# Router products placed singly between value products, and other orders in the opening and the first expert, of a gated cross-attention and mixture-of-experts layer in f32

## The chip, the cores and the metric

One core of a Trainium2 chip runs the whole layer in one program. The metric is the device time of one execution in microseconds (us); times of the kernel before are given as the median of three runs, and the profile is of one further execution.

## The reference

The layer has 4096 rows x of 512 features and a context of 3202 rows. First the rows are normalised and attend to the context by a trilinear similarity; the attended rows go through W_qv and are added to x by a gate. Then each row is normalised again, a router picks two of eight experts for it, and each expert is a two-layer network over at most 640 rows. All of it is f32.

```python
Sim  = (q @ w1)[:, None] + (ctx @ w2)[None, :] + (q * w3) @ ctx.T + b_sim   # q = layernorm(x)
hat  = softmax(Sim, axis=1) @ ctx
hbar = softmax(Sim.max(axis=1), axis=0) @ q
x    = x + tanh(g_xattn) * (concat([q, hat, q * hat, q * hbar]) @ W_qv + b_qv)
...
n = layernorm(x)
gates = softmax(n @ w_router + b_router);  topv, topi = top_k(gates, 2)
buf[e, pos] = n[token]        # each expert's rows, first come, up to its capacity
out = gelu(buf @ w1[e] + b1[e]) @ w2[e] + b2[e]
y   = weighted mean of the two experts' rows;  x + tanh(g_ffn) * y
```

## The kernel before

Every matrix product of size goes by the seven products of Strassen and Winograd: sums of blocks are formed on VectorE (DVE), seven products are done on TensorE (PE) into PSUM banks, and their results are combined on DVE and ScalarE (ACT). A function that does so has a chain of products named 1, 6, 7, 5, 2, 4, 3 in that order. The engines run in an order that the tile framework's scheduler records for each of them; `tc.issue_after(x)` holds an instruction behind another in that order, and a DMA belongs to the order of the engine that issues it (SyncE, called SP, for most loads; ACT and GpSimd, called POOL, for some).

**Attention.** Eight groups of 512 rows are worked one after the other. For the first group `stage_a_first` (L183 to L205) loads four tiles of 128 rows, normalises each (`layernorm`, L94: statistics on DVE, the reciprocal root `rstd` on POOL, the norm on DVE), transposes them on PE (L111), copies them by ACT (L192), and scales them into Qp on DVE (L197); `right_sums` (L176 to L179) forms the block sums of the right side. At the kernel's start stand also two iotas on POOL with casts on DVE, `tok` and `sno` (L79 to L86), which are used only in routing and by the experts. `tok_i` and `sno_i` share one buffer.

`stage_s` makes the scores of a group: for each of 7 pairs of context blocks (the last is a pair of 65 rows) the chain at L399, with its products at L453. In the first group `build` (L314) loads each block of the context (ktb, 896 KB with its sums), forms its block sums on DVE and stores it (L327, from ACT) for the other groups, which load it from there. `live["norm"]` (L202) and `live[0]["t2"]` are the instructions behind which these sums are held. The end of stage_s finds the greatest score of each row: transposes of M on PE (mps, L477), the reduction mt, a diagonal matrix dgm, a product with ones (mbps, L155), which puts the maxima along the free dimension of all partitions, and the copy mb on ACT (L495). `stage_e` subtracts mb from the scores (L510) and exponentiates them (L511).

`stage_v` makes the value products (L570). In the first group they are not by the seven products: for each half i of the features and each half h of the context there are 26 products of 512 columns. In between, DVE and POOL work on what later groups need: `build_values` (values' block sums, stored to memory) and `build_weights(c)`, which loads W_qv's parts, forms their sums and stores them, one c after each (i, h). Four products with a column of ones follow (rsps, L655), then the second group's scores (`pas`, `p6s` and so on). `xr`, loaded on SP at the end of stage_v's preparations for `stage_d`, holds rows of x.

**Router products.** Before the first group's values the kernel folds the router's weights into W_qv: for each of the four parts k of W_qv, 16 products of 128x128 with 128x8 (`router_weights`, L250), each of which is two records in the trace, since it is in f32. Part 1 stands before mps, part 2 after mbps, and parts 0 and 3 after all value products. The parts of W_qv lie in buffers lent by others: wq1 in hqT's, wq2 in xr's, wq0 in hs2's and hs4's, wq3 in T2's. The products of parts 1 and 2 go to PSUM bank we12 and those of 0 and 3 to we03; DVE copies them to `we` (L580, L600, L601).

**Routing** (L844 to L1094): products (L912), norms, choice of experts, positions by products with a triangular matrix (L1014), and 64 indirect scatters from POOL (L1045) that put each normalised row in its expert's rows of `buf_d`. `out` is stored by ACT (L920) ahead of the statistic Square (L923).

**Experts** (L1102 to L1322): `expert_in(e)` (L1164) loads five tiles xb of 128 rows from buf_d, each as soon as one of three buffers is free, transposes them on PE (bps, L111), copies them on DVE to bT (L1179), takes each row's factor and token number (dc, cf, ti, L1183 to L1186) and forms the block sums x (L1190 to L1193). The first expert's row loads wait for all scatters. `w1_sums` and `w2_sums` form the weights' block sums w1s (L1126 to L1129) and w2t (L1210 to L1213); `seven` (L1131) does the products pah, p6h, p7h and so on (L1135). `expert_in` and `w1_sums` of the next expert stand in the middle of the one before.

## Time and profile before

| what | value |
|---|---|
| time of the kernel before, median of 3 runs | 2696.91 us (2695.22 to 2697.17) |
| profiled execution, its own time | 2696.22 us |
| span of that execution in the profile | 2694.4 us |
| busy share of PE, DVE, ACT, POOL | 98%, 62%, 17%, 9% |
| mean granted clock of PE in the span | 0.987 |
| mean rate of the DMA | 162 GB/s |

The profile gives the engines' busy times, the span in 40 slices of 67.4 us, the groups of instructions by line with the idle time ahead of them, and who ended it. PEclk and "granted clock" are the share of full speed at which PE was allowed to run. A line of the timeline gives the start from the beginning of the span, the length, the engine, the line in the code, the operation, and the names of the tiles that it writes and reads; x32 at its end says that 32 records in a row were put together, and brackets tell the idle time ahead and what ended it. A matmul in f32 is two records, so 32 records are 16 matmuls. PEld is the load of weights into PE, which may run beside the products.

### The profile page before, as it was taken

How to read it: one execution, taken by the hardware profiler on the slowest of the kernel's cores; microseconds unless marked ns; L12 is line 12 of the kernel's file. 1: busy time of each engine (PE TensorE's matmuls, PEld its weight loads, DVE VectorE, ACT ScalarE, POOL GpSimd, SP SyncE). 2: the span in 40 equal slices, each digit the busy share in tenths (PEclk: the TensorE clock that was granted, in tenths of full speed). 3: DMA queues.
4: the chain of work that ended last, by engine and by line, in shares of the span. 5: the costliest groups of instructions: out<-in, count | busy, mean ns of one | idle time of the engine just before them, and what ended most of it. 6: DMA issues, size and time to landing. Idle time of an engine off the chain costs nothing. (4 is left out here: it accounts for less than half of the span.)

```text
span 2694.4 us, 29935 instructions
## 1 busy us (share of the span) xinstructions
PE 2644.3 (98%) x11388; PEld 2130.5 (79%) x11388; DVE 1671.4 (62%) x3283; ACT 449.6 (17%) x768; POOL 241.0 (9%) x292
## 2 busy tenths in 40 slices
PE   8999999999999999999999996999999999999999
PEld 6748888888888888888888875677777777777776
DVE  7765756845937757559357366564747475655654
ACT  1200200201201102002011043111121111111111
POOL 0210000000000000000000056001001010101010
PEclk9898999999999999999999998999999999999999
DMA  6885765656637647556446694323323132323210
GB/s 260 246 305 187 181 219 153 228 171 165 232 142 178 235 164 193 198 165 214 160 147 198 209 366 148 131 90 121 110 82 126 63 127 100 118 83 106 82 59 20
DMA packets 184051, 436.65 MB, mean 162 GB/s; under 512 B 18616, under 2 KB 85165, under 8 KB 181858
## 3 DMA queue, kind: packets, MB, share of 16 engines
q1 hardware_dynamic: 157538, 357.48, 41.3%
q0 software_dynamic: 16624, 47.37, 5.3%
q10 hardware_dynamic: 9744, 29.87, 2.9%
q8 instruction: 90, 1.47, 0.2%
q14 instruction: 55, 0.45, 0.1%
HBM read 356.22 MB, written 85.60 MB: 164 GB/s over the span
## 5 line engine op out<-in xcount | busy, mean ns | idle before, releaser
L453 PE MATMUL pas<-Qp,kt 128*128 128x256 f32 (+1 forms) x728 | 175.5, 383 | 0.0
L1135 PE MATMUL pah<-bT,w 128*128 128x320 f32 x512 | 161.0, 437 | 0.8 <-DVE bT L1179 0.8
L570 PE MATMUL pbv<-E,vt 128*128 128x256 f32 (+1 forms) x728 | 159.5, 379 | 0.0
L570 PEld LDWEIGHTS pbv<-E,vt 128*128 128x128 f32 (+1 forms) x728 | 138.2, 190 | 18.9
L453 PEld LDWEIGHTS pas<-Qp,kt 128*128 128x128 f32 (+1 forms) x728 | 136.0, 188 | 21.4
L511 ACT ACTIVATE E<-E 128x1024 f32<-128x1024 f32 (+1 forms) x112 | 110.7, 995 | 156.2 <-DVE E L510 154.3
L510 DVE TENSOR_TENSOR E<-E,mb 128x1024 f32<-128x1024 f32 (+1 forms) x112 | 124.7, 1138 | 12.4 <-ACT mb L495 12.4
L1135 PEld LDWEIGHTS pah<-bT,w 128*128 128x128 f32 x512 | 98.0, 192 | 39.9 <-DVE bT L1179 1.2
L1135 PE MATMUL pao<-w,h 128*128 128x256 f32 x512 | 121.0, 379 | 0.0
L1315 POOL DMA_INDIRECT out<-acc,ti x40 | 42.9, 1072 | 861.0 <-DVE acc L1314 861.0
L912 PE MATMUL x1p<-W,q2T 128*128 128x264 f32 x512 | 116.1, 387 | 0.0
L410 ACT COPY p1s<-pas 128x512 f32<-128x512 f32 (+1 forms) x56 | 31.1, 555 | 499.2 <-issue 256.5
L1292 PE MATMUL op<-w,h 128*128 128x512 f32 x256 | 113.7, 592 | 0.0
L471 DVE TENSOR_TENSOR M<-M,E 128x1024 f32<-128x1024 f32 (+1 forms) x96 | 109.0, 1135 | 6.7 <-ACT p1s L410 0.5
L1135 PEld LDWEIGHTS pao<-w,h 128*128 128x128 f32 x512 | 96.7, 190 | 16.7 <-issue 4.3
L912 PEld LDWEIGHTS x1p<-W,q2T 128*128 128x128 f32 x512 | 96.7, 190 | 16.1
L426 DVE TENSOR_TENSOR E<-p4s,u3s 128x512 f32<-128x512 f32 (+1 forms) x56 | 36.5, 652 | 109.8 <-PE p4s L453 109.8
L522 DVE TENSOR_TENSOR SM<-SM,E 128x1024 f32<-128x1024 f32 (+1 forms) x80 | 88.5, 1106 | 0.0
L1292 PEld LDWEIGHTS op<-w,h 128*128 128x128 f32 x256 | 47.2, 190 | 52.0 <-issue 46.4
L453 PE MATMUL p6s<-q,kt 128*128 128x256 f32 (+1 forms) x364 | 87.3, 381 | 0.0
L453 PE MATMUL pbs<-Qp,kt 128*128 128x256 f32 (+1 forms) x364 | 86.6, 379 | 0.0
L453 PE MATMUL pbs<-q,kt 128*128 128x256 f32 (+1 forms) x364 | 86.6, 379 | 0.0
(406 smaller groups left out, 5245.7 us busy)
## 6 DMA issues: line engine op xcount, KB each, us to landing
kt<-kt_d SPq DMA_DIRECT2D x84, 896.0 KB
w<-in_w SPq DMA_DIRECT2D x32, 2048.0 KB
wp<-wt_d SPq DMA_DIRECT2D x56, 520.0 KB
vt<-vs_d SPq DMA_DIRECT2D x28, 896.0 KB
vt<-vs_d SPq DMA_DIRECT2D x28, 640.0 KB
kt_d<-ktb ACTq DMA_DIRECT2D x12, 896.0 KB
buf_d<-zero SPq DMA_DIRECT2D x80, 129.0 KB
xb<-buf_d SPq DMA_DIRECT2D x40, 258.0 KB
```

The lines of the kernel that those rows point to most:

```text
L410: nc.scalar.copy(p1, cut(pa))
L426: tt(done(1, 0), cut(p4), u3, ALU.add)
L453: nc.tensor.matmul(ps[:w, jl, :], kts[j][:, KSLOT[p], k, :], B[p][:, k, :], start=start and jl == 0 and k == 0, stop=stop and k == 1, skip ...
L471: tt(m, m, e[:w, :, h], ALU.max)
L510: live[g]["last"] = tt(e, e, m, ALU.subtract)
L511: live[g]["exp"] = nc.scalar.activation(e, e, AF.Exp)
L522: tt(s, E_t[0][:, lr] if jj == 1 else s, e, ALU.add)
L570: mm = nc.tensor.matmul(ps[b], vt[: WJ[j], j - i * JH, b * P : (b + 1) * P], right(j), start=start and j == 0 and (b == 0 or g == 0), stop ...
L912: mm = nc.tensor.matmul(ps[:, j, :B1], qTs[g][:, c, q * P : (q + 1) * P], W1[:, c, j, :], start=(c == 0), stop=(c == DC - 1))
L1135: nc.tensor.matmul(ps, a, b, start=start and i == 0, stop=stop and i == len(A) - 1, skip_group_check=True)
L1292: nc.tensor.matmul(ps, hT[:, k, 2 * MH :], W2[:, k, :], start=(k == 0), stop=(k == KH - 1))
L1315: sc = nc.gpsimd.indirect_dma_start(out=out[:, :], out_offset=rows_of(ti, s), in_=acc[:, :], in_offset=None, bounds_check=N - 1, oob_is_er ...
```

## The change

The iota and cast of `tok` go to routing, those of `sno` to the beginning of the experts' part. In `layernorm` the statistics are ordered behind the norm of the tile two before, and each tile's root behind that of the one before. Half of the scalings into Qp go to ACT, `live["norm"]` becomes the last scaling of the first two tiles, the first p1 copies are ordered behind the scalings, and the stores of the context blocks stand behind the chain of their pair. The router products become a generator of single products: one is issued after each value product, those of parts 1 and 2 through the first half i and those of parts 0 and 3 through the second, with both banks held from the start of stage_v; `build_weights` is called for no c, 0 and 1, 2, and 3 after the four (i, h). In routing the store of `out` stands behind Square. For the experts the first weight sums come before `expert_in(0)`, whose small operations stand behind them; five row tiles have buffers of their own; and every other copy to bT is done by ACT.

```diff
@@ -76,33 +76,29 @@
-    tok_i = const.tile([P, NT], I32, name="tok_i", tag="tok_i")
-    nc.gpsimd.iota(tok_i, pattern=[[P, NT]], base=0, channel_multiplier=1)
-    tok = const.tile([P, NT], F32, name="tok")
-    nc.vector.tensor_copy(tok, tok_i)
-    sno_i = const.tile([P, E * NST], I32, name="sno_i", tag="tok_i")
-    nc.gpsimd.iota(sno_i, pattern=[[P, E * NST]], base=0, channel_multiplier=1)
-    sno = const.tile([P, E * NST], F32, name="sno")
-    nc.vector.tensor_copy(sno, sno_i)
-
...
+    scales, normed = [], []
+
...
         st = sm.tile([P, 6], F32, name=f"st{t}", tag="st")
-        nc.vector.bn_stats(st, src)
+        with tc.issue_after(normed[-2]) if len(normed) > 1 else ExitStack():
+            nc.vector.bn_stats(st, src)
         mv = sm.tile([P, 2], F32, name=f"mv{t}", tag="mv")
...
         ve = sm.tile([P, 1], F32, name=f"ve{t}", tag="ve")
-        nc.gpsimd.tensor_scalar(ve, mv[:, 1:2], EPS, None, ALU.add)
-        nc.gpsimd.tensor_tensor(rstd, ve, neghalf, ALU.pow)
+        with tc.issue_after(scales[-1]) if scales else ExitStack():
+            nc.gpsimd.tensor_scalar(ve, mv[:, 1:2], EPS, None, ALU.add)
+        scales.append(nc.gpsimd.tensor_tensor(rstd, ve, neghalf, ALU.pow).ins)
         nc.gpsimd.tensor_tensor(sd[:, t : t + 1], ve, rstd, ALU.mult)
-        return nc.vector.tensor_scalar(dst, src, mv[:, 0:1], rstd, ALU.subtract, ALU.mult)
+        nrm = nc.vector.tensor_scalar(dst, src, mv[:, 0:1], rstd, ALU.subtract, ALU.mult)
+        normed.append(nrm.ins)
+        return nrm
@@ -187,19 +183,24 @@
                 nc.sync.dma_start(q, x[t * P : (t + 1) * P, :])
-                nrm = layernorm(sm, q, q, t)
+                layernorm(sm, q, q, t)
                 ps = transposed(ps_tr, q, f"qps{t}")
...
                     for c in range(DC):
-                        ts(Qp[:, c, h], qT[:, c, h], ws[:, 2 * DC + c : 2 * DC + c + 1], ws[:, DC + c : DC + c + 1], ALU.mult, ALU.add)
+                        w3, w2 = ws[:, 2 * DC + c : 2 * DC + c + 1], ws[:, DC + c : DC + c + 1]
+                        if c < DC // 2:
+                            qp = ts(Qp[:, c, h], qT[:, c, h], w3, w2, ALU.mult, ALU.add)
+                        else:
+                            live["qp"] = nc.scalar.activation(Qp[:, c, h], qT[:, c, h], AF.Identity, scale=w3, bias=w2)
+                    if t == 1:
+                        live["norm"] = qp
                 if t == 2:
...
                         nc.scalar.dma_start(bqv, b_qv.partition_broadcast(P))
-            live["norm"] = nrm
             right_sums(0, qT, Qp)
@@ -242,18 +243,20 @@
-            def step(ps, ks, first=True):
+            def products(ps, ks):
+
...
                                     ps[:, k, (f0 // P) + f, :], a[:, d, f * P : (f + 1) * P], wrc[:, d, :],
-                                    start=first and k == ks[0] and f0 == 0 and f == 0 and d == 0, stop=d == DC - 1,
+                                    start=k == ks[0] and f0 == 0 and f == 0 and d == 0, stop=d == DC - 1,
                                     skip_group_check=True,
...
-
-            return step
+                                yield
+
+            return products
@@ -324,7 +327,6 @@
                 tt(A21, A11, A21, ALU.subtract)
-            nc.scalar.dma_start(kt_d[j], kt)
             return kt
@@ -407,7 +409,8 @@
             p1 = tmp("p1")
-            nc.scalar.copy(p1, cut(pa))
+            with tc.issue_after(live["qp"].ins):
+                nc.scalar.copy(p1, cut(pa))
             p6 = bank(f"p6{name}")
@@ -458,6 +461,9 @@
                 e_add = chain(f"s{g}_{jj}", prod, w, nj, lambda i, j: e[:w, j, i, :, :])
+                if g == 0:
+                    for j in js:
+                        nc.scalar.dma_start(kt_d[j], kts[j])
                 m = M[:w, :, :nj, :]
@@ -470,18 +476,14 @@
             if g == 0:
-                rw, rps = router_weights(), we_bank("we12")
-                rw(rps, [1])
+                live[g]["we"] = router_weights()
             ps = ps_tr.tile([P, 4, P], F32, name=f"mps{g}", tag="tr")
...
             ps = ps_tr.tile([P, 4, P], F32, name=f"mbps{g}", tag="tr").rearrange("p a b -> p (a b)")
-            dr = diag_rows(ps, f"m{g}", mt)
-            if g == 0:
-                with tc.issue_after(dr.ins):
-                    rw(rps, [2], False)
+            diag_rows(ps, f"m{g}", mt)
@@ -494,8 +496,6 @@
             live[g]["mt"], live[g]["mb"] = mt, mb
-            if g == 0:
-                live[g]["we"] = rw, rps
@@ -562,7 +562,7 @@
-            def product(ps, what, right, start=True, stop=True):
+            def product(ps, what, right, start=True, stop=True, beside=iter(())):
                 for i in range(2):
@@ -572,33 +572,37 @@
                             )
+                            with tc.issue_after(mm.ins):
+                                next(beside, None)
                 return mm
...
             if g == 0:
-                rw, rps = v["we"]
-                with tc.issue_after(v["last"].ins):
-                    nc.vector.tensor_copy(we[:, 1:3], rps[:, 1:3])
+                ps12, ps03 = we_bank("we12"), we_bank("we03")
+                w12, w03 = v["we"](ps12, [1, 2]), v["we"](ps03, [0, 3])
                 for i in range(2):
...
                     for h in range(2):
-                        vv = product(
-                            ps, (h, i * 256), lambda j: E[j // 2][: WJ[j], :, h, j % 2, :], start=h == 0, stop=h == 1
+                        product(
+                            ps, (h, i * 256), lambda j: E[j // 2][: WJ[j], :, h, j % 2, :], start=h == 0, stop=h == 1,
+                            beside=w03 if i else w12,
                         )
+                        if (i, h) == (0, 1):
+                            assert next(w12, 0) == 0
+                            with tc.issue_after(v["last"].ins):
+                                nc.vector.tensor_copy(we[:, 1:3], ps12[:, 1:3])
                         for j in range(NJ)[(2 * i + h) * 4 : (2 * i + h + 1) * 4]:
...
                         with tc.issue_after(v["last"].ins):
-                            build_weights(2 * i + h)
+                            for c in [[], [0, 1], [2], [3]][2 * i + h]:
+                                build_weights(c)
                         if (i, h) == (0, 1):
...
                         nc.scalar.copy(hqT[:, 2 * i + b, :], ps[b].rearrange("p a b -> p (a b)"))
-                with tc.issue_after(vv.ins):
-                    rps = we_bank("we03")
-                    rw(rps, [0])
-                    rw(rps, [3], False)
-                    nc.vector.tensor_copy(we[:, 0], rps[:, 0])
-                    nc.vector.tensor_copy(we[:, 3], rps[:, 3])
+                assert next(w03, 0) == 0
+                nc.vector.tensor_copy(we[:, 0], ps03[:, 0])
+                nc.vector.tensor_copy(we[:, 3], ps03[:, 3])
                 between()
@@ -869,6 +873,11 @@
+        tok_i = c2.tile([P, NT], I32, name="tok_i")
+        nc.gpsimd.iota(tok_i, pattern=[[P, NT]], base=0, channel_multiplier=1)
+        tok = c2.tile([P, NT], F32, name="tok")
+        nc.vector.tensor_copy(tok, tok_i)
+
@@ -917,12 +926,13 @@
             )
-            nc.scalar.dma_start(out[t * P : (t + 1) * P, :], x1)
             junk = sb.tile([P, D], F32, name=f"jx{t}", tag="jx", bufs=2)
-            nc.scalar.activation(
+            sq = nc.scalar.activation(
                 junk, x1, AF.Square, scale=-float(D), bias=s.sum[:, i : i + 1], accum_out=s.ssd[:, i : i + 1]
             )
+            with tc.issue_after(sq.ins):
+                nc.scalar.dma_start(out[t * P : (t + 1) * P, :], x1)
@@ -1112,6 +1122,11 @@
+        sno_i = cb.tile([P, E * NST], I32, name="sno_i", tag="sno_i")
+        nc.gpsimd.iota(sno_i, pattern=[[P, E * NST]], base=0, channel_multiplier=1)
+        sno = cb.tile([P, E * NST], F32, name="sno", tag="sno")
+        nc.vector.tensor_copy(sno, sno_i)
+
@@ -1126,7 +1141,7 @@
             tt(S4, A12, S2, ALU.subtract)
-            tt(A21, A11, A21, ALU.subtract)
+            return tt(A21, A11, A21, ALU.subtract)
@@ -1161,12 +1176,12 @@
-        def expert_in(e):
+        def expert_in(e, after=None):
             xT = cb.tile([P, DC, CAP], F32, name=f"bT{e}", tag="bT")
...
             for s in range(NST):
-                xb = sb.tile([P, R], F32, name=f"xb{e}_{s}", tag="xb", bufs=3)
+                xb = sb.tile([P, R], F32, name=f"xb{e}_{s}", tag="xb", bufs=NST)
                 ld = nc.sync.dma_start(xb, buf_d[e * CAP + s * P : e * CAP + (s + 1) * P, :])
@@ -1176,14 +1191,16 @@
                 ps = transposed(ps_tr, xb, f"bps{e}_{s}")
-                nc.vector.tensor_copy(xT[:, :, s * P : (s + 1) * P], ps)
+                (nc.scalar.copy if s % 2 else nc.vector.tensor_copy)(xT[:, :, s * P : (s + 1) * P], ps)
...
                 dc = sb.tile([P, 1], F32, name=f"dc{e}_{s}", tag="dc")
-                tt(dc, xb[:, D : D + 1], xb[:, D + 1 : D + 2], ALU.subtract)
-                tt(c, xb[:, D + 3 : D + 4], sno[:, k : k + 1], ALU.is_equal)
+                with tc.issue_after(after.ins) if after else ExitStack():
+                    tt(dc, xb[:, D : D + 1], xb[:, D + 1 : D + 2], ALU.subtract)
+                    tt(c, xb[:, D + 3 : D + 4], sno[:, k : k + 1], ALU.is_equal)
                 nc.vector.scalar_tensor_tensor(c, dc, c, xb[:, D + 1 : D + 2], ALU.mult, ALU.add)
-                nc.vector.tensor_copy(ti[:, s : s + 1], xb[:, D + 2 : D + 3])
+                with tc.issue_after(after.ins) if after else ExitStack():
+                    nc.vector.tensor_copy(ti[:, s : s + 1], xb[:, D + 2 : D + 3])
@@ -1200,7 +1217,7 @@
             S1, S2, S4 = (cb.tile([P, 2, P * KQ], F32, name=f"w1s{k}_{e}_{h}", tag=f"w1s{k}") for k in (1, 2, 4))
-            left_sums(S1, S2, S4, A11, A12, A21, A22)
+            last_sum[0] = left_sums(S1, S2, S4, A11, A12, A21, A22)
             return A11, A12, A22, S1, S2, A21, S4
@@ -1214,10 +1231,11 @@
         stored = []
-        nxt = expert_in(0)
+        last_sum = [None]
+        w1s = w1_sums(0, 0)
+        nxt = expert_in(0, last_sum[0])
         with tc.issue_after(row_loads[-1]):
             load_half(0, 1)
-        w1s = w1_sums(0, 0)
         for e in range(E):
```

## The prediction

> **What bounds it now.** I read the page's busy shares first: TensorE (PE) has 98% of the span, so time can only come out of PE's idle gaps, its slow-clock stretches, or its work. Next the PE rows of the slices.
> ```profile
> span 2694.4 us, 29935 instructions
> PE   8999999999999999999999996999999999999999
> PEclk9898999999999999999999998999999999999999
> ```
> PE dips in slices 1 and 25, the clock in slices 2, 4 and 25: the opening, both ends of the first value products, and routing with the first expert. The view of waits names the gaps (us in total, times, longest):
> ```profile
> PE bps L111 <- DMA xb<-buf_d: 16.2, 1, 16.2
> PE qps L111 <- DVE q L105: 11.2, 2, 10.7
> PE mbps L155 <- DVE dgm L154: 1.5, 1, 1.5
> ```
> The chain of waits follows only the last scatters (12% "issue") and says nothing about these places; PE's own timeline does (start, length, idle before).
> ```profile
> 99.15 3.63 PE L250 MATMUL we<-wrc,wq 128*128 128x8 f32 x32
> 104.78 2.07 PE L155 MATMUL mbps<-dgm,ones 128*128 128x512 f32 x2 [1.51 <-DVE dgm L154]
> 106.65 6.83 PE L250 MATMUL we<-wrc,wq 128*128 128x8 f32 x32
> ...
> 204.90 12.17 PE L250 MATMUL we<-wrc,wq 128*128 128x8 f32 x64
> 216.92 1.84 PE L655 MATMUL rsps<-ones,mb 128*128 128x1 f32 x8
> 218.63 3.76 PE L453 MATMUL pas<-Qp,kt 128*128 128x256 f32 x8
> ```
> The router products are 64 matmuls, each two records: 22.6 us in three runs. In the last, 32 matmuls take 0.38 us each; in the first, 16 take 0.227. The windows say why (stretch, us, busy time of PE, PEld, DVE, ACT, POOL, granted clock, DMA share, GB/s): the clock is halved from 104.1 to 117.8 and from 206.5 to 223.6.
> ```profile
> 104.10:113.30 9.20, 8.52 (x34) 7.49 (x35) 6.71 (x9) 4.81 (x5) 0.38 (x1) 0.50 1.07 350
> 113.30:117.80 4.50, 4.50 (x7) 1.92 (x8) 4.50 (x5) 1.06 (x1) 3.08 (x1) 0.50 1.07 356
> 206.50:216.90 10.40, 10.40 (x51) 10.40 (x51) 3.62 (x10) 0.00 (x0) 1.60 (x3) 0.50 0.79 277
> 216.90:223.60 6.70, 6.70 (x21) 5.71 (x22) 5.80 (x10) 0.59 (x1) 0.66 (x1) 0.50 0.65 242
> 1560.00:1640.00 80.00, 76.03 (x343) 63.29 (x342) 49.24 (x253) 34.51 (x82) 46.69 (x52) 1.00 0.91 337
> ```
> A run of 128x8 products, though PE is "busy" through it, is followed by the half clock.
>
> **The sum** is made against the profiled execution: 2696.22 us, 1.8 outside its span, 0.7 below the median of 2696.91.
>
> **Opening.** Before, the first rstd (POOL, 9.53) stands behind the sno iota, which waits for the tok cast, which DVE does only after the fourth tile's bn_stats (8.52). With the iotas gone the early norms no longer wait for it. The last tile's own chain is bn_stats to 9.21, aggregate 0.18, ve 0.22, rstd 0.56, norm 0.55, with a hand-over of 0.1 to 0.3 between engines; I place its norm at 11.8 instead of 13.62. Then half of the Qp scalings (DVE, 0.33 each, 2.67 us in all) go to ACT, so the first x-sum starts near 15.1 instead of 18.00, and p6, which needs it, at 17.9 instead of 20.1 (its 21.81 less one product of 1.73 that now stands elsewhere in the order): −2.2. From 19.98 to 47.19 PE did 15 products of 1.727, 25.9 us of work in 27.2; the missing 1.3 is one p1 copy that ACT does at 40.80, 18.2 us late, because six kt_d stores of blocks not yet loaded stood before it. In the new order two do, of loaded blocks: −1.3. Together −3.5; between −1.5 (half, if the ktb loads, 896 KB per block, set the pace) and −5.5 (a clock step of 2 us as well).
>
> **Router products.** First place: from the end of the scores (99.31) to the first value product (113.33) there were 14.0 us. The softmax chain left there, by its rows: last max 1.4, transposes 0.6, mt 0.7, dgm 0.7, mbps 1.1 to 2.07 (1.6), mb copy 0.6, first subtraction 1.1, first exp 1.1, with 1.0 for the hand-overs: 8.8, so −5.2. In i = 0 go 32 matmuls at 0.22: a second row for it is the other 128x8 group, which stands between scores:
> ```profile
> 62.36 0.68 PE L453 MATMUL pbs<-q,ktb 128*128 128x256 f32 x2
> 62.87 0.51 PE L225 MATMUL beps<-wrc,dgb 128*128 128x8 f32 x4
> 63.23 0.68 PE L453 MATMUL pbs<-q,ktb 128*128 128x256 f32 x2
> ```
> The scores' own pace is 0.216 a record (1.727 for 8), so two of the 0.88 us from the row's start to that of the next but one, 62.36 to 63.23, are 0.43 of scores, and the four small records took 0.44: 0.22 a matmul. So +7.2. The value products start at half clock and wait for the release: 4.5 us at half lost 2.2; one step of 3.4 lost is half of it plus phase, and I take 2.55: +0.35. Second place: the run of 204.90 to 216.92 goes, −12.0; 32 matmuls in i = 1 come, +7.2; the half clock after it, 6.7 us doing 3.5 us of work plus rsps at 0.9 instead of 1.84, −3.3. Sum: −5.2 + 7.2 + 0.35 − 12.0 + 7.2 − 3.3 = −5.75, taken as −5.8. Bounds: between value products two, one or three weight loads of 0.11 (3.73 us of PEld for 35) may stay uncovered, the next product's among them; 64 times ∓0.11 is −7 or +7. The 0.224 stands between products too, so it is the nearest row, but both ends are kept: −12.8 to +1.2.
>
> The chain of the first stretch is now idle time, some 6 us of it without products. The trace shows that the run at 99.15 did not hold the clock: it fell at 104.1. The Trainium skill, page "TensorE: Matmul & The Clock Gate", section "Why this matters for your kernels", says to keep PE free of idle gaps beyond about 3 us; by that rule taking the run away would cost a step of half clock at the value products, some 1.7 us more, which the trace speaks against, as that step was paid already. No term here uses it.
>
> New waits: we03's PSUM bank is wanted by the second group's "5" product, about 216.4 in the old time. It must wait for the two copies of we, which stand on DVE behind the last weight sums. That pipeline (17 loads, sums and stores, about 4.9 us each, paced by the DMA; `wc` waits of 4.86 show it) ends near 211, with 4 us either way, so it is covered by 5 us; beyond that each us costs one. The xr load (1 MB) shares a buffer with wq2 and moves on SP's queue from 113 to some 141, behind the last w12 product; kt loads of the second group move behind the wc loads, and both still land before their use. The x-row sums behind the we copy on DVE wait for PE at 141.5, when DVE gets there at 143.9. These I cost at nothing.
>
> **Routing.** Square no longer stands behind its store's issue (0.34): the statistic and thus the last scatter come so much earlier: −0.35, within ±1, as DVE's order of choose and place is otherwise reshuffled. The tok iota and cast (0.16 each) are hidden under the value products.
>
> **First expert.** These rows carry it:
> ```profile
> 1676.58 0.98 POOL L1045 DMA_INDIRECT buf_d<-xn,sidx  x1 [0.30 <-issue]
> 1681.87 3.09 PE L111 MATMUL bps<-ident,xb 128*128 128x128 f32 x12 [16.21 <-DMA xb<-buf_d]
> 1685.74 2.50 PE L1135 MATMUL pah<-bT,w 128*128 128x320 f32 x4 [0.78 <-DVE bT L1179]
> 1693.64 1.45 PE L1135 MATMUL p6h<-x,w1s 128*128 128x320 f32 x4 [1.85 <-DVE x L1191]
> 1699.75 1.24 PE L1135 MATMUL pah<-bT,w 128*128 128x320 f32 x4
> ```
> The first row load still lands at 1681.8: the 64 scatters, 1.28 us apart, end there. Then five loads at once instead of three; before, the fourth and fifth land at 1687.9 and PE takes their transposes at 1688.03 and 1689.98. Now five sets of transposes (about 1.0 each at half clock) run to 1686.6, copies alternating between DVE (0.69) and ACT (0.59); x-sums end at 1689.2, four pah products run to 91.0, and p6h follows without its 1.85 wait, at 1691.0 instead of 1693.64: −2.6. From 1694.7 to 1698.2 the clock was half again after the gap, 1.7 us lost: gone. Sum −4.4 with rounding. DVE first waits for the sno cast, hence for POOL's iota behind the last scatter (1677.9), with three weight sums of 1.22 behind it; they end at 1682.7, when the copies begin: nothing. Bounds: −2 (the clock drops all the same) to −5.5.
>
> A second rule of that page, section "Part 4: PE-mode transpose", says that transposes do not count as PE-busy; by it the release would come up to 1.2 us later than I have it. The row from 1681.8 to 1691.3, half clock with 8.62 us of transposes and products, cannot tell.
>
> **Later experts.** Two of five bT copies go from DVE (0.68) to ACT (0.59), both covered by products; 0, or at worst 0.5 for seven experts, +3.5.
>
> Sum: −3.5 − 5.8 − 0.35 − 4.4 = −14.05; 2696.2 − 14.0 gives **2682.2**, and with half of the 0.7 to the median **2682.5 us**.
>
> **Rivals.** (1) Half gain. The weight pipeline ends late, PE waits for the we03 bank and falls to half clock again for a step or two (4.5), and the opening is paced by its loads (2): 14 less 6.5, about 2689 (2687 to 2693). For it: the pipeline's end is uncertain by 4 us against 5 of cover, and the DMA share there is 0.79. Against: the copies read banks whose products end before 200. Chance 0.19. (2) The change of place saves nothing: each router product costs 0.38 wherever it stands, as in the last run. 64 times 0.16 is 10.2 more: 2682.5 + 10.2 = 2692.7. Against: the row at 62.87, and that the 0.38 was at half clock. Chance 0.06. (3) Slower. 128x8 products lower the clock even among value products. The half clock after each run of them speaks for it. 32 value products of 0.858 (52 take 44.6) with 32 router products of 0.224 make 34.6 us; at half clock they cost as much again: one half of the value products so gives 2717, both 2752. It decides as soon as 14 of 34.6 us, 40% of one half, stay slow. Against: in the window of 1560 to 1640, groups of small products and waits come every 15.9 us and leave PE some 60% dense for 3.4 us, and the clock stays at 1.00; value products hold 79% (0.858 of 1.082) of the interleaved stretch. Chance 0.06.
>
> **The numbers.** Forecast 0.69; case 1 0.19; case 2 0.06; case 3 0.06. The range goes down to 2675, where the lower end of the router products (−7) alone would bring it, and up to 2690.5, which takes in their upper end (2689.5) and most of case 1; cases 2, 3 and the rest of 1 are left out. A measurement tells 0.2%, 5.4 us, from no change: faster means below 2691.5. The forecast and 0.16 of case 1 lie there, 0.85; the rest of case 1 and case 2 make 0.09; case 3, 0.06.
>
> **What would show it.** No half clock in the profile after from 206 to 223; first value product near 105; each i of value products 7 us longer; PE without a wait for we03's bank; p6h 2.5 us earlier behind the first transposes. A clock of 0.5 inside the value products, or a wait of the pbs product for the we copy, would make me wrong.

## The result and the profile after

The changed kernel takes 2680.72 us (median of 4 runs, 2680.40 to 2681.07) against 2696.73 of the kernel before (4 runs beside it): a ratio of 0.9942 with a 95% interval of 0.9924 to 0.9959. In a second comparison on one chip with two other kernels it took 2682.14 (5 runs, 2679.20 to 2683.20) against 2696.41: 0.9943, 0.9929 to 0.9956. The forecast was 2682.5, the range 2675 to 2690.5.

First the page, then the view of waits (us in total, times, longest) of the changed kernel. (Line numbers are now those of the changed file: L107 are transposes, L252 router products, L456 scores, L570 value products, L1150 the experts' products.)

```profile
span 2679.0 us, 29957 instructions
PEclk9999999999999999999999998999999999999999
```

```profile
PE bps L107 <- DMA xb<-buf_d: 15.0, 1, 15.0
PE qps L107 <- DVE q L99: 6.5, 2, 6.3
PE vv L570 <- ACT E L511: 3.0, 1, 3.0
PE pbs L456 <- DVE E L424: 2.0, 1, 2.0
```

Slices 2 and 4 no longer dip. Two waits are new: the value products for the first exponentials (3.0, where the router products stood), and a product of the scores for a sum on DVE (2.0). PE's timeline around the value products shows the shape of the change:

```profile
100.11 2.07 PE L151 MATMUL mbps<-dgm,ones 128*128 128x512 f32 x2 [1.51 <-DVE dgm L150]
105.20 2.07 PE L570 MATMUL vv<-E,vt_(0_0)_0_846 128*128 128x512 f32 x2 [3.02 <-ACT E L511]
107.07 0.43 PE L252 MATMUL we<-wrc,wq 128*128 128x8 f32 x2
...
111.83 0.28 PE L252 MATMUL we<-wrc,wq 128*128 128x8 f32 x2
111.97 1.10 PE L570 MATMUL vv<-E,vt_(0_0)_0_846 128*128 128x512 f32 x2
112.91 0.28 PE L252 MATMUL we<-wrc,wq 128*128 128x8 f32 x2
...
200.99 10.46 PE L570 MATMUL vv<-E,vt_(1_256)_1_1167 128*128 128x512 f32 x24
211.29 0.95 PE L659 MATMUL rsps<-ones,mb 128*128 128x1 f32 x8
212.11 1.97 PE L456 MATMUL pas<-Qp,kt 128*128 128x256 f32 x8
```

From one router product to the next is 1.08 us (111.83 to 112.91), of which a value product takes 0.858 (200.99 to 211.29 for the last 12): 0.22 for the router product. Nothing waits between the last value product and the second group's scores. The windows (stretch, us, busy time of PE, PEld, DVE, ACT, POOL, granted clock, DMA share, GB/s) show the clock:

```profile
99.90:105.20 5.30, 2.07 (x2) 0.50 (x2) 2.81 (x6) 1.64 (x2) 1.07 (x1) 0.50 1.06 356
105.20:110.10 4.90, 4.90 (x9) 2.69 (x10) 4.90 (x5) 4.23 (x4) 0.00 (x0) 0.50 1.09 342
110.10:142.40 32.30, 32.30 (x121) 17.98 (x120) 24.58 (x33) 8.69 (x12) 9.71 (x6) 1.00 0.57 181
...
159.50:211.30 51.80, 51.80 (x170) 26.92 (x169) 22.66 (x61) 1.17 (x2) 10.43 (x14) 1.00 0.90 301
211.30:218.00 6.70, 6.70 (x36) 6.02 (x35) 6.26 (x8) 1.17 (x2) 0.00 (x0) 1.00 0.91 307
```

Around the value products half clock remains only from 99.9 to 110.1; both interleaved stretches and the second group's first scores run at 1.00.

The whole is best read as a table of stages, from PE's timeline of each profiled execution. The 2nd profile of the changed kernel is that of after_again. Stage 1 ends with the first group's scores, 2 with the first value product, 3 with the last one, 4 with the second group's p7s, 5 with the first x1p of routing, 6 with the last x1p, 7 with the first row transposes of the first expert, 8 with its second p6h, 9 with the last product.

| kernel | 1 | 2 | 3 | 4 | 5 | 6 | 7 | 8 | 9 |
|---|---|---|---|---|---|---|---|---|---|
| before | 99.3 | 14.0 | 91.7 | 19.6 | 1308.5 | 125.0 | 23.8 | 20.0 | 986.0 |
| changed | 96.4 | 8.8 | 106.3 | 4.2 | 1309.1 | 123.6 | 22.5 | 15.1 | 986.5 |
| difference | -2.9 | -5.3 | +14.5 | -15.4 | +0.7 | -1.4 | -1.3 | -4.9 | +0.5 |
| changed, 2nd profile | 99.1 | 8.8 | 106.0 | 4.2 | 1309.1 | 123.6 | 22.6 | 14.9 | 986.5 |
| router_only | 101.5 | 7.8 | 105.5 | 4.2 | 1308.5 | 125.0 | 23.8 | 21.2 | 985.9 |
| runs8 | 97.2 | 8.8 | 105.8 | 4.2 | 1308.5 | 127.9 | 23.8 | 16.0 | 986.5 |
| runs16 | 97.6 | 8.5 | 113.4 | 4.2 | 1308.5 | 126.3 | 23.9 | 15.4 | 986.5 |
| runs32 | 96.4 | 8.2 | 116.9 | 4.2 | 1308.5 | 129.0 | 23.6 | 16.0 | 986.5 |
| holes | 99.5 | 8.8 | 101.8 | 4.2 | 1310.1 | 123.8 | 23.8 | 15.7 | 986.5 |
| warm | 97.4 | 7.8 | 103.8 | 4.2 | 1308.5 | 123.4 | 23.8 | 15.7 | 986.5 |
| open | 97.4 | 11.3 | 106.3 | 4.2 | 1308.5 | 128.1 | 23.7 | 16.0 | 986.5 |
| xb3 | 97.2 | 8.5 | 106.7 | 4.2 | 1309.1 | 123.6 | 23.8 | 22.6 | 986.5 |
| store | 96.0 | 7.8 | 105.5 | 4.2 | 1309.1 | 125.4 | 22.6 | 15.7 | 986.5 |
| dvecopy | 97.5 | 8.8 | 106.2 | 4.2 | 1309.2 | 123.6 | 22.7 | 14.6 | 987.5 |
| mix | 96.5 | 7.8 | 101.4 | 4.2 | 1308.5 | 123.5 | 22.6 | 15.9 | 986.5 |

The differences of the third row add up to -15.5; the spans differ by 15.4. The rows below also tell what one profile is worth. Stages 1 and 7 vary among kernels that do the same there (96.0 to 99.5; 22.5 to 22.7 or 23.6 to 23.9), so nothing under 2 us is read from their lengths alone, and a total of an edited kernel is not compared where the edit concerns one stage: small edits shift the scheduler's order elsewhere (in stage 6 of runs8, runs16, runs32 and open PE waits once 2.7 to 2.9 us for DVE, in all but runs16 with half clock behind it). The totals of the kernels that were run once: runs8 2686.86 us, runs16 2692.43, runs32 2697.39, holes 2682.55, warm 2679.36, open 2690.21, xb3 2690.42, store 2681.18, dvecopy 2682.49.

### The profile page after: what moved, and what is told of

Its sections match the earlier page's. It is cut to its first block, busy times and chain, and to the rows that moved or that the text cites. A ratio compares the mean times of both kernels' runs of the same rounds, so it can differ in the third digit from the quotient of the medians.

```text
span 2679.0 us, 29957 instructions
## 1 busy us (share of the span) xinstructions
PE 2630.3 (98%) x11388; PEld 2117.3 (79%) x11388; DVE 1661.0 (62%) x3263; ACT 462.3 (17%) x788; POOL 237.6 (9%) x292
## 5 line engine op out<-in xcount | busy, mean ns | idle before, releaser
L456 PE MATMUL pas<-Qp,kt 128*128 128x256 f32 (+1 forms) x728 | 173.7, 380 | 0.0
L1150 PE MATMUL pah<-bT,w 128*128 128x320 f32 x512 | 159.1, 433 | 0.5 <-ACT p1h L1157 0.5
L570 PE MATMUL pbv<-E,vt 128*128 128x256 f32 (+1 forms) x728 | 159.5, 379 | 0.0
L570 PEld LDWEIGHTS pbv<-E,vt 128*128 128x128 f32 (+1 forms) x728 | 138.2, 190 | 18.9
L456 PEld LDWEIGHTS pas<-Qp,kt 128*128 128x128 f32 (+1 forms) x728 | 134.9, 186 | 21.0
L1150 PEld LDWEIGHTS pah<-bT,w 128*128 128x128 f32 x512 | 97.4, 191 | 39.8 <-ACT p1h L1157 1.0
L1150 PE MATMUL pao<-w,h 128*128 128x256 f32 x512 | 120.9, 379 | 0.0
L1150 PEld LDWEIGHTS pao<-w,h 128*128 128x128 f32 x512 | 97.3, 190 | 20.1 <-issue 7.7
L426 ACT COPY E<-pas 128x512 f32<-128x512 f32 (+1 forms) x56 | 31.0, 554 | 329.7 <-PE pas L456 316.1
L456 PE MATMUL p6s<-q,kt 128*128 128x256 f32 (+1 forms) x364 | 86.6, 379 | 0.0
L456 PE MATMUL p4s<-q,kt 128*128 128x256 f32 (+1 forms) x364 | 86.6, 379 | 0.0
L456 PE MATMUL p7s<-Qp,kt 128*128 128x256 f32 (+1 forms) x364 | 86.6, 379 | 0.0
## 6 DMA issues: line engine op xcount, KB each, us to landing
buf_d<-zero SPq DMA_DIRECT2D x80, 129.0 KB
```

The source lines that it names most:

```text
L456: nc.tensor.matmul(ps[:w, jl, :], kts[j][:, KSLOT[p], k, :], B[p][:, k, :], start=start and jl == 0 and k == 0, stop=stop and k == 1, skip ...
L570: mm = nc.tensor.matmul(ps[b], vt[: WJ[j], j - i * JH, b * P : (b + 1) * P], right(j), start=start and j == 0 and (b == 0 or g == 0), stop ...
L1150: nc.tensor.matmul(ps, a, b, start=start and i == 0, stop=stop and i == len(A) - 1, skip_group_check=True)
```

## The experiments

**router_only.** The kernel before with the router part of the diff only (the hunks of `router_weights`, the end of `stage_s` and `stage_v`).

> The kernel before with the router products' part of the change alone. If the parts add up as the two traces show them (5.3 us less between the end of the first scores and the first value product, 14.5 more in the value products, 15.4 less between their end and the second group's p7s), it takes 6.1 us less than before, about 2690.6 us, and the opening and the first expert stay as they were. If the router products cost the same wherever they stand and the gain comes from the other parts alone, it stays at 2696 to 2697. If the parts help one another (the clock's steps fall otherwise in each start of the first scores), it lies outside 2689 to 2692.

Measured: 2686.84 us (6 runs, 2685.69 to 2691.68) against 2695.60, a ratio of 0.9967 (0.9955 to 0.9980): 8.8 us less, with 5.4 to 12.1 by the interval. The second theory, no gain, falls. The profiled execution is the slowest of the six (2691.68): its granted clock starts at 24.3 us, not at 18.8, which makes stage 1 2.2 longer by chance. Stages 2 to 4 together give -7.8: the half clock fell on the first value products for one step only (109.6 to 113.1). So in the stages the sum of 6.1 is right within what the place of the clock's steps moves: half clock for one step instead of three explains the other 1.7. The totals do not settle it. The median of 2686.84 lies outside the 2689 to 2692 that adding up allowed, on the side of more gain, and the four fastest runs lie 4.2 us or more under the profiled one and were not profiled themselves. By the totals (16.0 and 14.3 for the whole change) 5.5 to 7.2 would be left for the other parts, where their stages give 9.3. Whether the parts add up therefore stays open; that the router products bring a gain by themselves is shown.

**runs8, runs16, runs32.** The same number of router products, ended behind the same value product, but in runs of G = 8, 16 and 32:

```diff
-                            with tc.issue_after(mm.ins):
-                                next(beside, None)
+                            done.append(mm)
+                            if len(done) % G == 0:
+                                with tc.issue_after(mm.ins):
+                                    for _ in range(G):
+                                        next(beside, None)
```

> The changed kernel with the router products in runs of 8 (1.8 us) behind every eighth value product instead of singly, the same number, ended at the same value product. Theory: the clock falls where large products hold too small a share of a stretch of some 3.4 us; before, 2.0 of 3.4 us of value products (203.1 to 206.5) ended in half clock, singly 79% did not. Runs of 8 leave 47% in the worst stretch, so some of the eight runs are followed by half clock of 3.4 us or more, each 1.7 us at least: 2 to 15 us slower than the changed kernel. First rival, only a whole stretch without a large product counts: no change, 2680.7. Second rival, router products count like any product and the half clock of before had another cause: no change here or with longer runs.

> The same with runs of 16 (3.6 us at full clock) behind the 16th and 32nd value product of each half. Theory of the share: each of the four runs brings half clock for 3.4 to 6.8 us: 7 to 16 us slower than the changed kernel. First rival (a whole stretch without a large product): at most one or two of four fall, 0 to 5 us. Second rival: no change.

> The same with one run of 32 (7.1 us at full clock) behind the 32nd value product of each half. Theory of the share and first rival alike: the run goes to half clock within 1.6 to 3.4 us, as the run at 204.9 did, and the value products behind it start at half clock: 5 to 8 us for each, 10 to 16 us slower than the changed kernel. Second rival: no change, 2680.7, and then what counts is only that the run stood behind the last value product.

Measured in stage 3, where alone they differ on purpose: 105.8, 113.4 and 116.9 against 106.3. Eight runs of 8 cost nothing (the 6.1 us more in the total, 2686.86, are stages 6 to 8); runs of 16 cost 7.2, runs of 32 10.6. Here is the first run of 16, then the step of the clock in which it begins, the two steps behind that one, and the step of a later run in the same kernel that kept the clock:

```profile
122.77 4.33 PE L252 MATMUL we<-wrc,wq 128*128 128x8 f32 x32
```

```profile
122.10:125.50 3.40, 3.40 (x28) 2.92 (x27) 3.04 (x5) 3.40 (x5) 0.00 (x0) 1.00 0.13 28
125.50:132.30 6.80, 6.80 (x16) 3.70 (x16) 6.80 (x12) 1.23 (x2) 1.32 (x2) 0.50 0.39 87
180.10:183.50 3.40, 3.40 (x25) 2.68 (x23) 1.75 (x5) 0.00 (x0) 0.76 (x1) 1.00 0.93 373
```

PE is busy through all of them. In 122.1 to 125.5 value products hold 20% (0.7 of 3.4 us), and the clock is 0.50 for the next two steps; in 180.1 to 183.5 they hold 34%, and it stays. Two of the four runs fell, the two whose steps held 20% and 25%; the others held 34% and 41%. In runs32 both fell (0% and 28%), in runs8 none of eight (the worst step is left 50%). So for these runs a step's share of large products decides, as the theory has it, but the bound lies near 30%, not above 50% as I had expected, and the place of the run within the 3.4-us steps decides as much as its length. The first rival, that only a step without any large product counts, falls with the steps of 20, 25 and 28%; the second falls with runs16 and runs32.

**holes.** 18 router products moved into PE's idle time of stage 2:

```diff
+                for _ in range(6):
+                    next(w12)
             ps = ps_tr.tile([P, 4, P], F32, name=f"mps{g}", tag="tr")
...
+                with tc.issue_after(tr.ins):
+                    for _ in range(6):
+                        next(w12)
...
+                with tc.issue_after(dr.ins):
+                    for _ in range(6):
+                        next(w12)
```

> The changed kernel with 18 of the 64 router products put where PE idles in the softmax chain ahead of the first value product: 6 before mps, 6 between mps and mbps, 6 behind mbps; the others stay singly. Theory (a router product beside value products costs 0.22 us of PE, an idle PE costs nothing): the end of the scores to the first value product stays 8.8 us, within 0.5, and the value products take 18 x 0.22 = 4.0 less than their 106.3. Rival: they delay the chain, at half clock 0.43 each, as the run ahead of mps did in the kernel before (mps 3.3 us behind the scores, not 1.5); then the first stretch grows by 1 to 4 us and eats the gain.

Measured: stage 2 8.9, stage 3 101.8, 4.4 less than the changed kernel. The theory holds; the rival's delay is 0.1. The total of 2682.55 hides it, since stage 1 came out at 99.5 and stage 7 at 23.8.

**warm.** Extra products in the same idle time, from a tile that is loaded anyway into a PSUM bank that nobody reads:

```diff
+                heat(512, 256)
             ps = ps_tr.tile([P, 4, P], F32, name=f"mps{g}", tag="tr")
...
+                with tc.issue_after(tr.ins):
+                    heat(512, 256)
...
+                with tc.issue_after(dr.ins):
+                    heat(512, 512, 512)
```

> The changed kernel with extra products of 256 and 512 columns, whose results nobody reads, in the idle time of the softmax chain: 0.86 + 0.43 us before mps, the same before mbps, 3 x 0.86 behind it. In the run kernels the clock fell when large products held 0 to 28% of a stretch of 3.4 us and not at 34% and more. Theory: idle time of PE ahead of the value products is what brought the half clock (99.9 to 110.1), so with these it stays at full: mbps 1.0 us shorter, and the first 5 us of value products lose nothing: 3.4 us less from the end of the scores to the end of the value products. Rival: the extra products delay the chain by what they save, or the clock falls all the same: within 0.7 us of the changed kernel there.

Measured: stages 2 and 3 take 111.65 us against 115.02, 3.37 less, for 3.4 expected. Its windows beside those of the changed kernel above:

```profile
97.40:105.20 7.80, 6.92 (x21) 2.90 (x20) 5.36 (x10) 1.64 (x2) 0.94 (x1) 1.00 1.07 361
105.20:110.00 4.80, 4.80 (x17) 2.70 (x18) 4.80 (x5) 4.23 (x4) 0.00 (x0) 1.00 1.09 352
```

The clock does not fall here, and in 4.8 us at the start of the value products PE gets 17 records done where the changed kernel got 9 in 4.9. Its total, 2679.36, is under all but one run of the changed kernel. How much is saved depends on where the steps of the clock fall: in router_only and store, which have no extra products, only one step is at half clock, and their stages 2 and 3 take 113.3 together. Beside these `warm` saves 1.7.

**open.** The block sums of context blocks 4 and later stand behind the last-but-one sum of the chain before them:

```diff
-                        kts[j] = build(j)
+                        kts[j] = build(j, late if jj else None)
...
+            for sums in late:
+                with tc.issue_after(d10.ins):
+                    sums()
             return tt(done(0, 1), cut(pb), u2, ALU.add)
```

> The changed kernel with DVE's block sums of context blocks 4 and later put behind the third-but-last sum of the pair of scores before them, instead of ahead of that pair. Theory: the 2.0 us wait of the fourth pbs product (at 39.03, for a sum of scores) came from DVE standing in front of a block that had not landed; without it PE has no wait there and the scores end 2.0 us earlier, 94.4 instead of 96.4 (the start of the clock may shift it by 2). Rival: the loads set the pace, and PE waits as long for the blocks themselves, or for their sums at p6.

Measured: no gain; stage 1 ends at 97.4, 0.9 later than in the changed kernel (the clock starts at 14.7 and 14.6), and stage 2 grows by 2.5. The waits of PE:

```profile
PE mps L493 <- DVE M L488: 3.6, 1, 3.6
...
PE p6s L467 <- DVE ktb L328: 2.3, 1, 2.3
```

The wait for E is gone, PE has no gap up to 78, and then p6s waits 2.3 us at 80.63 for the sums themselves: the wait went to another name, as the rival has it. What held the sums at that moment was DVE's own order, not a load of a context block. PE has finished the p4 product at 74.7, but its sum on DVE, behind which the edit holds the block sums, stands behind statistics of rows of x, and these wait for their load:

```profile
76.16 1.31 DVE L278 BATCH_NORM_STATS2 st<-q 128x6 f32<-128x512 f32 x2 [1.55 <-DMA q<-in_x]
...
78.79 0.69 DVE L436 TENSOR_TENSOR E<-p4s,u3s 128x512 f32<-128x512 f32 x1
79.40 0.75 DVE L327 TENSOR_TENSOR ktb<-ktb 128x256 f32<-128x256 f32 x2
```

So the experiment exchanged one wait of DVE in order for another; it does not show what the scores would take if DVE never stood before a load. DVE's work at the end of the chain, 2.1 us more ahead of mps, is the edit's own price.

**xb3.** `tag="xb", bufs=3` instead of `bufs=NST`.

> The changed kernel with three buffers for the experts' row tiles instead of five, so that the fourth and fifth load wait for the first two to be used. Theory: these loads set the start of the first expert in the kernel before (transposes at 1688.0 and 1690.0); from the first row transposes to the second p6h it takes 2 to 5 us more than the 15.1 of the changed kernel, up to the 20.0 of before. Rival: the shared copies (ACT and DVE) and the earlier weight sums made the gain: within 0.5 us of 15.1. Later experts: no difference by either.

Measured: stage 8 takes 22.6, 7.4 more than the changed kernel and 2.5 more than before.

```profile
1673.08 1.94 PE L107 MATMUL bps<-ident,xb 128*128 128x128 f32 x8 [15.13 <-DMA xb<-buf_d]
1675.70 1.11 PE L107 MATMUL bps<-ident,xb 128*128 128x128 f32 x4 [0.69 <-ACT bT L1194]
1677.60 2.50 PE L1150 MATMUL pah<-bT,w 128*128 128x320 f32 x4 [0.78 <-DVE bT L1194]
...
1683.76 1.06 PE L107 MATMUL bps<-ident,xb 128*128 128x128 f32 x4
1687.39 1.52 PE L1150 MATMUL p6h<-x,w1s 128*128 128x320 f32 x4 [2.57 <-DVE x L1208]
```

The last transposes come 10.7 us behind the first, p6h waits again for the x-sums (2.6), and the clock is half once more (1688.4 to 1691.8). The theory holds, and by more than the upper end expected: with three buffers the rest of the change makes this stage worse than before. Five buffers with the old order of the weight sums were not run, so what they are worth by themselves is not shown.

**dvecopy.** `nc.vector.tensor_copy` for all copies to bT.

> The changed kernel with all copies to bT on DVE, none on ACT. Theory: five loads at once make the gain of the first expert; without ACT the five copies of 0.69 stand one behind the other on DVE with the small operations, and from the first row transposes to the second p6h it takes 0.5 to 2 us more than 15.1. Rival: the share of the copies matters more, 3 us or more; or it matters in later experts too: the stretch from the second p6h to the last product, 986.5 us, grows by up to 3.5.

Measured: stage 8 14.6, under the 14.9 to 16.0 of all kernels with five buffers and the changed copies; stage 9 987.5, 1.0 more. The view of waits behind the first expert's start has one row:

```profile
PE pbh L1150 <- DVE h L1268: 1.4, 1, 1.4
```

The theory falls in its own stage: ACT's copies gain nothing in the first rows. What they are good for is one wait later, of which the rival's bound of 3.5 was too wide: 1.0.

**store.** The store of `out` ahead of Square on ACT, as before.

> The changed kernel with the store of out ahead of Square on ACT again, as before, in the routing. Theory of the prediction: only the last Square is late by the store's issue, 0.34 us more in the stretch from the last x1p to the first row transposes (22.5 to 23.9 in the runs so far). Rival: the order also made the groups of x1p shorter (15.50 us from one to the next against 15.93 before, where PE waited 0.6 for rv or oh): then they go back to 15.93, about 3 us in the seven groups.

Measured: stage 6 takes 125.4 against 123.6, with the groups of x1p at 15.93 again (once 16.21). Of store and then of the changed kernel, the same product of a group:

```profile
1592.56 0.41 PE L1023 MATMUL pos<-mask,upper 128*128 128x32 f32 x2 [0.59 <-DVE mask L1005]
```

```profile
1592.90 0.41 PE L1024 MATMUL pos<-mask,upper 128*128 128x32 f32 x2 [0.15 <-DVE mask L1006]
```

PE waits 0.56 to 0.60 (once 0.87) in each of six groups, against 0.11 to 0.16; the changed kernel in turn has one wait of 0.83 at 1640.53 that store has not. So the rival holds, with 1.8 us for the 3 expected. The edit is one instruction's place on ACT, and what it moved is when DVE has the mask for PE ready.

Stage 7 is 22.6 in both. The 0.34 of the prediction is nevertheless there: the last Square starts 1.22 us behind the last x1p in store, 1.24 in the kernel before, and 0.89 in the changed kernel. Behind it stand the last scatters on POOL, and one of them takes longer than the usual 0.97, in the changed kernel and in the kernel before; in store none does. In the changed kernel (first row; then the kernel before) that eats most of the 0.34:

```profile
1659.10 1.27 POOL L1055 DMA_INDIRECT buf_d<-xn,sidx  x1 [0.30 <-issue]
```

```profile
1669.19 1.96 POOL L1045 DMA_INDIRECT buf_d<-xn,sidx  x1 [0.30 <-issue]
```

**mix and after_again.** The best of the above in one kernel, beside the changed kernel itself: 11 router products and four extra products (0.43 + 3 x 0.86 us) in stage 2.

```diff
+                fold(4)
+                heat(256)
             ps = ps_tr.tile([P, 4, P], F32, name=f"mps{g}", tag="tr")
...
+                    fold(2)
+                    heat(512)
...
+                    fold(4)
+                    heat(512)
+                    fold(1)
+                    heat(512)
```

> The changed kernel itself, beside the kernel before and the mixed one on one chip. Its four runs so far lie at 2680.4 to 2681.1; the profiles of its relatives differ by up to 3 us in the opening (where the granted clock starts) and 1.3 us in the last scatters, so 2679 to 2683, 13 to 16 us under the kernel before, is expected.

> The changed kernel with both fillings of the idle time ahead of the first value product: 11 router products there (4 before mps, 2 before mbps, 5 behind it) and extra products of 256 and 512 columns between them, so that large products hold at least about 36% of any 3.4 us. If both effects add (holes: 0.22 us for each router product; warm: 3.4 us of half clock gone), the stretch from the end of the scores to the end of the value products is 3.4 + 11 x 0.22 = 5.8 us shorter than the changed kernel's 115.0, and the whole about 2675. Rival: router products take the share under what holds the clock (it fell at 0 to 28%, held at 34 to 46%), the half clock comes back, and only 2.4 us, or nothing, are gained.

Measured: after_again 2682.14 (2679.20 to 2683.20); mix 2675.80 (5 runs: four from 2675.10 to 2676.24, one 2683.48) against 2696.41, a ratio of 0.9929 (0.9916 to 0.9943). Stages 2 and 3 take 109.2 against 115.0: 5.8 less, as expected, so both effects add (beside the 113.3 of router_only and store it is 4.1 less).

```profile
96.50:104.40 7.90, 7.33 (x38) 4.32 (x36) 5.46 (x10) 1.65 (x3) 0.60 (x1) 1.00 1.05 351
104.40:109.00 4.60, 4.60 (x17) 2.67 (x18) 4.60 (x5) 4.22 (x4) 0.00 (x0) 1.00 1.08 359
```

By the medians it is 6.3 us under the changed kernel; the two intervals against before overlap, so the stages carry this claim more than the totals do. What the one run of 2683.48 met was not profiled.

## Why the prediction was right, step by step

**Opening**, forecast -3.5: the size is right, two of its steps are not. The early norms went as said, and more: p6 starts at 16.1, not 17.9. The other step, "the missing 1.3 is one p1 copy ... because six kt_d stores of blocks not yet loaded stood before it", named the wrong owner. With the stores moved, the same place waits 2.0:

```profile
39.03 1.99 PE L456 MATMUL pbs<-Qp,ktb 128*128 128x256 f32 x8 [1.97 <-DVE E L424]
```

In the changed kernel DVE idles 3.76 us ahead of 32.5 and 1.56 ahead of 36.2 for loads of context blocks, with the sums of scores behind them in its order; before, it idled 5.26 ahead of 38.8 for such a load, the stores on ACT stood behind that, and the p1 copy was what showed it. The wait is read off whichever instruction stands last in such a row. `open` took it away there and met another one at p6s, for a load of x. I had this as the lower end (-1.5, "if the ktb loads set the pace"). In the eleven profiles that have this opening with its order left alone, stage 1 ends between 96.0 and 99.5, against 99.3 and 101.5 in the two with the old one, so about 3 us is what can be said. Which of the opening's edits made it was not taken apart by a run.

**Router products**, forecast -5.8: measured -5.3 + 14.5 - 15.4 = -6.1 in the profiles (rounded), and alone -7.8 in the stages and -8.8 in the total. The chain of 8.8 us was 8.8; the matmul of 0.224 was 0.222; no drop behind the value products, 15.4 for 15.3. The steps that were bounds became measurements: the ends of 0.11 and 0.33 for one matmul are excluded. The new wait for the bank of we03 is covered: DVE's copies end at 209.5 (forecast 211), and pbs starts at 217.4, 7.9 us later. Rival 2 (0.38 wherever they stand) falls with this row, rival 1 with the missing wait.

**Rival 3**, half clock among value products, did not happen, and the runs show how far off it was: with 79% of value products in the mixture it had a wide margin over the 30% or so under which runs of them lowered the clock. The argument from the window of 1560 to 1640 (about 60% dense, clock 1.00) was sound. What I wrote at its head, that a run of 128x8 products "is followed by the half clock", is true only where the run leaves a step of 3.4 us less than some 30% of large products; of eight runs of 1.8 us none was followed by it.

**Routing**, forecast -0.35: it came out at -2.7 in the two profiles, and the step was in the wrong place. 1.4 is in the groups of x1p, from the recorded order (shown by `store`); the 1.3 of stage 7 has two parts before the forecast one is even seen. The kernel before and router_only lose 1.0 by one scatter of nearly 2 us. Of the twelve profiles with the whole change, five take 22.5 to 22.7; in the other seven DVE's last sum of x1p starts 1.1 us later, for a reason that was not looked for, and they take 23.6 to 23.9, as before. So the change's own share of it is not shown, beyond the 0.34 at the Square. Half a microsecond of a wait of x1p for the output sums (0.5, in stage 5) went the other way and had not been foreseen.

**First expert**, forecast -4.4: measured -4.9. Without five loads at once the gain is gone (`xb3`), as the prediction put it; the alternating copies, which it counted in, do not make it (`dvecopy`). **Later experts**, forecast 0, bound +3.5: +0.5, and the ACT copies there save 1.0 that all-DVE copies would cost.

**The total**, forecast 2682.5, measured 2680.72 and 2682.14: the main terms were right for the reasons given, but that the total is so close is partly luck. The opening alone differs by 2.7 between two profiles of the changed kernel, and the 2.3 that routing gave beyond its forecast is of about the size of what stages 5 and 9 lost and the opening fell short, 1.8 together.

Of the rules weighed from the Trainium skill's "TensorE: Matmul & The Clock Gate", the one of its section "Why this matters for your kernels", no idle gaps of PE beyond about 3 us, warned rightly of this chain, and I was too quick to set it aside: the half clock that comes from the idle time of stage 2 costs 3.4 us in the changed kernel, as `warm` shows. But the gaps are shorter than the rule has it: the clock falls at 99.9, ahead of the wait of 3.02, after a step of 3.4 us in which PE was busy for 0.66 and no wait was longer than 1.5. Against the kernel before it cost nothing more, since the run at 99.15 did not hold the clock either (half from 104.1 to 117.8, now from 99.9 to 110.1), which is why the sum did not suffer. The one of "Part 4: PE-mode transpose", that transposes do not count as busy, is contradicted here, for transposes in f32. In this window of the changed kernel, counting only the transposes (us, busy PE, PEld), they hold 3.02 of 3.40 us at half clock, and the clock is full from 1676.9. In the second profile they hold 2.96, with 0.1 of other products, and the clock is full from 1679.1. In the kernel before, 2.89 us of transposes (12.0 to 15.4) brought no full clock yet, and 2.92 us of score products (15.4 to 18.8) did, so both seem to count alike.

```profile
1673.40:1676.80 3.40, 3.02 (x12) 2.28 (x12) 0.50 1.00 398
```

## What to carry to other kernels

Small products cost their own 0.22 us and nothing else here when each stands beside a large one; gathered in runs of 3.6 us and more they brought the half clock upon themselves and upon what follows in four of six cases, though the engine never stopped. Before an idle stretch ahead of a long stage is accepted, fill it: with work that is due anyway, and with large products for the clock; here that was worth 4.1 to 5.8 us, not much less than the whole move of the router products. When a wait vanishes in a rewritten order, ask which load or sum stood behind it: a wait named after an in-order engine's last instruction can come back under another name.

## What the runs showed of the hardware

- The granted clock changes in steps of 3.41 us, and in these traces what it does follows what PE did in the step just ended. With runs of 128x8 products in it, it fell where large products held 0, 20, 25 and 28% of the step, and stayed at 34, 41 and 50%. One fall does not fit by plain time: at the end of the value products before (203.1 to 206.5) they held 52%. Nearly all of that were products of 65 rows, and counted by half they make 27%, but no run tests such a count. Where PE idled instead, it also fell at 45%: in the second profile of the changed kernel the wait of the opening left 1.53 us of 3.40, and one step of half clock followed (40.7 to 44.1, 2.7 us later at the end of stage 1 than in the first profile, with the later start of the clock). Among the other steps with idle time some kept it at 42 to 53% busy (xb3, 36.4 to 39.8; store, 97.4 to 100.8) and some lost it at 38 to 53% (holes, 37.4 to 40.8; open, 1581.4 to 1584.9), so the bound is not sharp, or more than busy time counts.

```profile
37.30:40.70 3.40, 1.53 (x8) 1.02 (x7) 3.33 (x8) 0.00 (x0) 0.00 (x0) 1.00 0.74 308
40.70:44.10 3.40, 3.40 (x10) 2.68 (x9) 1.88 (x3) 0.00 (x0) 0.00 (x0) 0.50 0.93 330
```

- To get back to full clock takes more than to keep it: in runs16 and runs32 steps at half clock stayed there with 43 to 64% of large products and router products in the rest (125.5 to 128.9: 58%), where the same mixture at full clock held it from 34% on.
- The place of these steps differs from one execution to the next: the clock starts between 14.5 and 17.1 us in the changed opening, and stage 2 takes between 7.8 and 8.8 with one and the same code, 7.8 where mbps falls into a step at full clock and 8.8 where all of it is at half.
